# Two adds of a graph attention kernel move from VectorE to GpSimd

## The chip, the cores and the metric

The kernel runs on one core of a Trainium2 chip. A core has TensorE (PE: matmuls, with its weight loads shown apart as PEld), VectorE (DVE), ScalarE (ACT), GpSimd (POOL) and SyncE (SP, which here only issues DMAs). Each engine works through its own queue of instructions in order, and semaphores tie the queues together. The metric is the device time of one execution in microseconds; lower is better.

## The reference

Two graph layers are applied to 64 independent graphs of 256 nodes with 512 features, all in float32. Layer 0 is a one-head graph attention with a leaky ReLU; layer 1 is an 8-head attention whose scores carry a bias and the logarithm of the adjacency. Both add their input at the end.

```python
# layer 0
feat_proj = einsum('bnh,oh->bno', feats, fc_w) + fc_b
q = einsum('bnh,oh->bno', feat_proj, q_w) + q_b
k = einsum('bnh,oh->bno', feat_proj, k_w) + k_b
masked = q + swapaxes(k, 2, 1) + (1.0 - adj_mat) * -1e9
masked = where(masked >= 0, masked, 0.01 * masked)
x = einsum('bnm,bmh->bnh', softmax(masked), feat_proj) + feats
# layer 1: 8 heads of 64
Q, K, V = (x @ W + b for each of q, k, v)
scores = einsum('bihd,bjhd->bhij', Q, K) / sqrt(64)
a, c = x @ w_g[:D], x @ w_g[D:]
scores = scores + (a[:, :, None] + c[:, None, :] + b_g + log(adj + 1e-9))[:, None]
out = einsum('bhij,bjhd->bihd', softmax(scores), V) + x
```

## The kernel before, in words

The 64 graphs are taken in 32 groups of two (512 tokens). The work is a software pipeline of steps: in a step, group F goes through layer 0 and the projections of layer 1, group A, one older, goes through the attention of layer 1, group D, two older, finishes its last output, and the next group X loads and prepares its layer-0 weights. A steady step takes about 71 us. The order of instructions on each engine is written out by hand: `step` and `attention_and_layer_0` are lists of piece names, and each piece issues its instructions in that place. Nothing is reordered later; the framework only adds the semaphore waits that data and buffers need. PSUM has four single banks, `bank`, and two pairs of banks, `pair`, for the scores.

Weights of the softmax in layer 1 are made transposed (keys on partitions), for one graph `gr` and four heads at a time, which is a unit `u` = 0 to 3. A unit has two tiles `e[u, 0]` and `e[u, 1]`, one for each half of the keys, each 128 x 1024.

- `scores` (L859, L873): matmuls, then the exponential on ACT writes `e`.
- `factor` (L879): DVE multiplies `e` by adjacency + 1e-9, which stands for the logarithm in the scores.
- `both` (L886): the unit's two tiles are added into `esum`, the line that the change touches first.
- `parts` (L916, L917): DVE turns `esum` in blocks of 32 x 32 and reduces it to partial sums, so that the softmax needs no pass of its own. `totals` (L927) finishes the sums by a small matmul, `ratios` (L942, L951) takes reciprocals. In the last step of all, `sums_1` (L962) takes the sums for graph 0 by matmuls that read `esum` themselves.
- `attend` (L899, L906): matmuls of `e` with the values, copied to SBUF by ACT; `turn` (L991) transposes them on DVE, `divide` (L1011) multiplies by the reciprocals, `complete` (L1019) adds the residual with the bias, `xb`, and `store` (L1049) sends the tile out on SP's DMA queue. The last two outputs of the kernel go through `finish` (L1033 to L1040) in place of these.

Each of the large products (`pf` for layer 0, `pq`, `pk`, `pv` for layer 1) is a two-by-two block scheme with seven products instead of eight (L412), so sums of blocks precede and follow it. Its pieces `p1` to `p7` are matmuls, `keep_1` and the ends of `p6` and `p5` copy a bank to SBUF on ACT, and `sum_00` to `sum_11` are DVE instructions which read a PSUM bank and one SBUF tile (L443; for `pf` L501). The product `pf` is special (class `Mixed`): its kept tiles get the residual added on POOL (L495), the only steady work of POOL. The sums of token blocks are `ysum:0` to `ysum:3` for `pf` (L350, tiles `tb`, after ACT has copied `yT`, L695), and `xsum` for the others (L375). `keys`, `dot_q` and `dot_k` (L519) are dot products of the features with a vector; both inputs are in SBUF. `send` (L793, L797) and `fetch` (L805) transpose the result of layer 0 through DRAM. `load_x` (L206) loads the next group's features into the one buffer of x, after `keys` has read it.

The places of the two pieces in the order: `both:0` and `both:1` follow the factors of unit 1 and come before `ysum:0`; `both:2` comes after `turn:0` and `ratios:0`; `both:3` after the factors of unit 3 and before the `keys`. `complete:1` stands between `divide:1` and `store:1`, ahead of `ysum:1`; `complete:0` after the `dot_q`, with `store:0` and `parts:2` behind it:

```python
A("factor:1:0 factor:1:1 pv.sum_10 both:0 both:1")
F("mix:0 mix:1 ysum:0 recip")
D("ratios_of_all divide:1 complete:1 store:1")
A("residual:1")
F("mix:2 mix:3 ysum:1 ysum:2 ysum:3")
A("parts:0")
F("pf.p1 pf.keep_1 pf.p2 pf.p6 pf.sum_00 begin send:0:0 fetch:0:0")
```

The buffers concerned: `esum` has two, `e` six, `osb` two (shared with the turned tile of `parts:0`), `xb` two.

Of the kernel before, what the change touches and what calls it, by code (L numbers as in the profile page):

```python
# [13 lines left out]
ALU = mybir.AluOpType  # L14
# [11 lines left out]
def kernel(  # L26
# [64 lines left out]
    nc = tc.nc  # L91
# [72 lines left out]
    def fast():  # L164
        main = ExitStack()
        with main:
# [112 lines left out]
            def constant():  # L279

                both = two.tile([P, NC], F32, tag="c", name="qk_col")
                part = two.tile([P, 2, T], F32, tag="kq", name="qk_fcb")
                nc.vector.tensor_tensor(both, qw_col, kw_col, ALU.add)
                nc.vector.tensor_tensor(both, both, fcb_col, ALU.mult)
                nc.vector.tensor_reduce(part[:, 0, 0:1], both, AX.X, ALU.add)
                pk = bank("pk")
                nc.tensor.matmul(
                    pk[:, 0:1], lhsT=part[:, 0, 0:1].to_broadcast([P, P]), rhs=ones[:, 0, 0:1],
                    start=True, stop=True,
                )  # L290
                return lambda: nc.vector.scalar_tensor_tensor(
                    kqc, pk[:, 0:1], qb, kb, ALU.add, ALU.add
                )
# [235 lines left out]
            class Group:  # L529
# [353 lines left out]

                def both(self, u):
                    self.esum[u] = two.tile([P, 2, 2, N], F32, tag="es", name=f"es_{self.g}_{u}")
                    nc.vector.tensor_tensor(self.esum[u], self.e[u, 0], self.e[u, 1], ALU.add)  # L886

                def attend(self, gr):

# [126 lines left out]
                    )  # L1016

                def complete(self, gr):
                    nc.vector.tensor_tensor(self.osb[gr], self.osb[gr], self.xb[gr], ALU.add)  # L1019

                def ratios_t(self, gr):
                    self.st = one.tile([P, N], F32, tag="sms1", name=f"st_{self.g}_{gr}")
# [383 lines left out]
```

## Time and profile before

| what | us |
|---|---|
| time, median of 3 runs | 2311.84 (2310.98 to 2312.35) |
| span of the profiled execution, first to last instruction | 2308.8 |
| median less span | 3.0 |
| PE busy | 2294.2 (99%) |
| DVE busy | 2124.2 (92%) |
| ACT busy | 1071.8 (46%) |
| POOL busy | 121.9 (5%) |
| `both`, 126 on DVE | 149.3 |
| `complete`, 62 on DVE | 75.6 |

The profile is of one execution. A row of a group gives line, engine, operation, output and inputs by the program's tile names, shapes and count; then busy time in us and mean ns of one; then the idle time of the engine ahead of it and what ended most of it. A row of the timeline gives start and duration in us, engine, line and operation; a bracket is idle time before it with what ended it. A row of the waits says who waited for whom: total us, times, longest. DVE instructions overlap by some hundredths of a microsecond at their ends, and the ends of matmuls are modelled.

### The profile page before, as it was taken

Reading aid. Unit: us, or ns where it says so; the run is one execution under the profiler, and the core shown is the slowest. Engines: PE = TensorE matmul, PEld = TensorE weight load, DVE = VectorE, ACT = ScalarE, POOL = GpSimd, SP = SyncE. Lnnn points to the kernel's source line nnn. Section 1 sums busy time; section 2 is a strip of 40 time slices with the busy share of each in tenths; the row PEclk is TensorE's granted clock in tenths of the full one; section 3 lists DMA queues with packets and bytes.
Section 4 is the critical chain, followed back from the end, with each engine's and each line's share of the span. In section 5 each row is a group of like instructions: output and inputs, shape, how many; then the busy total and the mean of one; then the engine's idle time right before and its main releaser. Section 6 shows DMA issues by size and latency. Waiting matters only on the chain.

```text
span 2308.8 us, 33613 instructions
## 1 busy us (share of the span) xinstructions
PE 2294.2 (99%) x12618; PEld 1905.2 (83%) x12618; DVE 2124.2 (92%) x3180; ACT 1071.8 (46%) x1865; POOL 121.9 (5%) x120
## 2 busy tenths in 40 slices
PE   9999999999999999999999999999999999999997
PEld 6888888888888888888888888888888888888885
DVE  6899999999999999999999999999999999999997
ACT  3544444454445444454444454444544445444443
POOL 0000000000000000000000000000000000000000
PEclk9999999999999999999999999999999999999999
DMA  4122332223322233232233232332222323223312
GB/s 133 46 61 73 78 76 66 70 61 85 79 73 61 61 78 78 74 68 61 69 78 83 60 75 63 79 78 74 64 60 74 78 73 70 65 64 81 84 46 38
DMA packets 517264, 163.84 MB, mean 71 GB/s; under 512 B 415188, under 2 KB 478696, under 8 KB 517096
## 3 DMA queue, kind: packets, MB, share of 16 engines
q1 hardware_dynamic: 514440, 160.32, 28.8%
q8 instruction: 102, 1.67, 0.3%
q10 hardware_dynamic: 2656, 1.31, 0.2%
q14 instruction: 66, 0.54, 0.1%
HBM read 95.43 MB, written 66.12 MB: 70 GB/s over the span
## 4 chain that ended last, share of the span: by engine, by line
PE 98%; DVE 1%; DMA 0%; ACT 0%; issue 0%; ACTq 0%; DVEq 0%
PE pv L412 17%; PE pq L412 17%; PE pf L412 16%; PE pk L412 16%; PE sc L859 11%; PE oT L899 10%; PE y L689 9%; PE fp L718 1%; DMA fc_nat<-in_L_gnn_fc_w_dram 0%; PE rc L637 0%; DVE osb L1034 0%; PE tot L927 0%; DVE osb L1040 0%; PE xTp L705 0%; DVE osb L1033 0%; DVE x L756 0%
## 5 line engine op out<-in xcount | busy, mean ns | idle before, releaser
L873 ACT ACTIVATE e<-sc,c 128x1024 f32<-128x1024 f32 x254 | 269.0, 1110 | 79.2 <-PE sc L859 77.6
L879 DVE TENSOR_TENSOR e<-e,am 128x1024 f32<-128x1024 f32 x254 | 297.7, 1213 | 0.4 <-ACT e L873 0.4
L859 PE MATMUL sc<-qT,kT 64*128 64x256 f32 x2048 | 255.8, 390 | 0.3 <-ACT e L873 0.3
L899 PE MATMUL oT<-e,v 128*64 128x256 f32 x2032 | 233.4, 382 | 0.0
L859 PEld LDWEIGHTS sc<-qT,kT 64*128 64x128 f32 x2048 | 187.3, 187 | 52.6 <-issue 32.7
L495 POOL TENSOR_TENSOR pf_s<-pf_s,x 128x512 f32<-128x512 f32 x93 | 118.4, 1273 | 2106.1 <-ACT pf_s L494 2038.8
L689 PE MATMUL y<-e,x 128*128 128x256 f32 x992 | 225.6, 381 | 0.0
L899 PEld LDWEIGHTS oT<-e,v 128*64 128x64 f32 x2032 | 140.2, 137 | 85.3 <-issue 10.7
L689 PEld LDWEIGHTS y<-e,x 128*128 128x128 f32 x992 | 186.4, 190 | 23.7
L432 ACT ACTIVATE pq_s<-pq,cols 128x256 f32<-128x256 f32 x192 | 80.5, 470 | 249.1 <-PE pq L412 249.1
L494 ACT ACTIVATE pf_s<-pf,recip 128x256 f32<-128x256 f32 x186 | 77.9, 470 | 197.6 <-PE pf L412 197.6
L917 DVE TENSOR_REDUCE part<-est 128x32 f32<-128x1024 f32 x124 | 151.3, 1220 | 4.3
L916 DVE STREAM_TRANSPOSE est<-es 128x1024 f32<-128x1024 f32 x124 | 152.2, 1227 | 0.0
L886 DVE TENSOR_TENSOR es<-e,e 128x1024 f32<-128x1024 f32 x126 | 149.3, 1205 | 1.1
L695 ACT COPY yT<-y 128x512 f32<-128x512 f32 x124 | 72.6, 585 | 131.7 <-PE y L689 130.9
L429 ACT COPY pk_s<-pk 128x512 f32<-128x512 f32 x96 | 56.3, 586 | 165.7 <-PE pk L412 159.0
L906 ACT COPY oTs<-oT 128x512 f32<-128x512 f32 x128 | 75.0, 586 | 118.0 <-PE oT L899 97.3
L412 PE MATMUL pk<-t1b,wk 128*128 128x256 f32 x512 | 121.1, 380 | 0.4 <-DVE kT L443 0.4
L412 PE MATMUL pv<-wv,t1b_c 128*128 128x256 f32 x512 | 121.1, 380 | 0.0
L412 PE MATMUL pv<-wv,t1b 128*128 128x256 f32 x512 | 121.0, 380 | 0.0
L412 PE MATMUL pq<-x1T,wq 128*128 128x256 f32 x512 | 121.0, 379 | 0.0
L412 PE MATMUL pk<-x1T,wk 128*128 128x256 f32 x512 | 121.0, 379 | 0.0
(181 smaller groups left out, 4506.3 us busy)
## 6 DMA issues: line engine op xcount, KB each, us to landing
x<-in_x_dram SPq DMA_DIRECT2D x32, 1024.0 KB, 5.1
out_dram<-osb SPq DMA_DIRECT2D x254, 128.0 KB, 3.1
xd<-xt SPq DMA_DIRECT2D x124, 256.0 KB, 2.0
x1T<-xd SPq DMA_DIRECT2D x496, 64.0 KB, 1.9
adj<-in_adj_dram SPq DMA_DIRECT2D x128, 128.0 KB, 3.5
qrow<-q SPq DMA_DIRECT2D x31, 256.0 KB, 3.9
fc_nat<-in_L_gnn_fc_w_dram ACTq DMA_DIRECT2D x4, 256.0 KB, 3.8
wq<-in_L_gnn_W_q_dram SPq DMA_DIRECT2D x1, 1024.0 KB
```

Of the source, the lines that this page charges most:

```text
L412: nc.tensor.matmul(o, lhsT=lk[:, ts(m, P)] if len(lk.shape) == 2 else lk[:, m], rhs=rk, start=(start and m == 0 and k == 0), stop=(m == 1 ...
L432: nc.scalar.activation(dst[:, m], src[:, m], AF.Identity, bias=self.bias[:, 2 * o + m : 2 * o + m + 1],)
L494: nc.scalar.mul(s[:, m], src[:, m], self.recip[:, TPG * k + m : TPG * k + m + 1])
L495: nc.gpsimd.tensor_tensor(s, s, self.out(o, k), ALU.add)
L689: nc.tensor.matmul(y[:, ts(gr, N)], lhsT=self.x[:, gr * TPG + j, ts(c, P)], rhs=self.e0[:, j, gr, :], start=(gr == 0 and j == 0), stop=(gr ...
L859: nc.tensor.matmul(sc[:, par, pr, :], lhsT=self.kT[rows, 2 * hg + pr, ts(t, P)], rhs=self.qT[rows, 2 * hg + pr, ts(gr, N)], start=True, st ...
L873: nc.scalar.activation(e, sc, AF.Exp, bias=self.c[:, t : t + 1], scale=SCALE)
L879: nc.vector.tensor_tensor(ef, ef, self.am[:, jc, u // 2, :].unsqueeze(1).to_broadcast([P, 4, N]), ALU.mult,)
L886: nc.vector.tensor_tensor(self.esum[u], self.e[u, 0], self.e[u, 1], ALU.add)
L899: nc.tensor.matmul(oT[par * HD : (par + 1) * HD, pr, :], lhsT=self.v[:, gr * TPG + jc, ts(h, HD)], rhs=self.e[2 * gr + hg, jc][:, par, pr, :],
L916: nc.vector.transpose(turned, self.esum[u].rearrange("p a b i -> p (a b i)"))
L917: nc.vector.tensor_reduce(self.part[:, hg, :], turned.rearrange("p (m c) -> p m c", c=B), AX.X, ALU.add,)
```

## The change

Two method bodies issue their add on GpSimd and no longer on VectorE. Everything else, the order of the pieces included, stays. `both` then sits in POOL's queue among the three adds of `pf` in a step: POOL's order is `both:0`, `both:1`, `complete:1`, the three adds of `pf`, `both:2`, `both:3`, `complete:0`.

```diff
 def both(self, u):
     self.esum[u] = two.tile([P, 2, 2, N], F32, tag="es", name=f"es_{self.g}_{u}")
-    nc.vector.tensor_tensor(self.esum[u], self.e[u, 0], self.e[u, 1], ALU.add)
+    nc.gpsimd.tensor_tensor(self.esum[u], self.e[u, 0], self.e[u, 1], ALU.add)
...
 def complete(self, gr):
-    nc.vector.tensor_tensor(self.osb[gr], self.osb[gr], self.xb[gr], ALU.add)
+    nc.gpsimd.tensor_tensor(self.osb[gr], self.osb[gr], self.xb[gr], ALU.add)
```

## The prediction

> **What bounds the kernel now.** The page was read first: busy time and the chain that ended last.
>
> ```profile
> PE 2294.2 (99%) x12618; PEld 1905.2 (83%) x12618; DVE 2124.2 (92%) x3180; ACT 1071.8 (46%) x1865; POOL 121.9 (5%) x120
> PE 98%; DVE 1%; DMA 0%; ACT 0%; issue 0%; ACTq 0%; DVEq 0%
> ```
>
> TensorE (PE) never rests and nearly the whole chain is PE behind PE. VectorE (DVE) is at 92%, close enough to be taken for a partner bottleneck, so the waits of PE were read next. All of them together:
>
> ```profile
> PE pok L1096 <- DVE okp_last L1065: 5.0, 1, 5.0
> PE warm L1176 <- POOL ones L214: 1.5, 1, 1.5
> PE x1Tp L811 <- DVE x L756: 0.5, 1, 0.5
> PE pk L412 <- DVE kT L443: 0.4, 1, 0.4
> PE sc L859 <- ACT e L873: 0.3, 1, 0.3
> ```
>
> Each of these occurs once (total, times, longest). In the 31 steady steps of some 71 us PE waits for nobody; the 5.0 us at the end are for the range check. So shorter DVE work by itself is worth about nothing: what it could save is the single 0.4 us. A PE busy time may hide gaps, so the spacing was looked at too: 16 matmuls of the product pf start at 1012.80 and the next 16 at 1016.25, 216 ns each at a granted clock of 0.997, and the other products look the same. The question is therefore only whether the change makes DVE late enough for PE to wait, and the timeline of one steady step answers where the slack is small.
>
> The groups by shape give the prices:
>
> ```profile
> L886 DVE TENSOR_TENSOR es<-e,e 128x1024 f32<-128x1024 f32 x126 | 149.3, 1205 | 1.1
> L1019 DVE TENSOR_TENSOR osb<-osb,xb 128x1024 f32<-128x1024 f32 x62 | 75.6, 1220 | 1.1
> L495 POOL TENSOR_TENSOR pf_s<-pf_s,x 128x512 f32<-128x512 f32 x93 | 118.4, 1273 | 2106.1 <-ACT pf_s L494 2038.8
> ```
>
> [...]during the 93 POOL adds DVE runs transposes, a reduction and the PSUM-reading L501, which keep their usual 1.20 to 1.24 us and 0.47 us, and the adds take 1266 to 1292 ns. [...]no DVE instruction with two SBUF inputs lies under a POOL add for more than 0.08 us. [...]doubling the 1273 ns gives 2.55. I take 2.4.
>
> **The change, part by part.** DVE loses 126 x 1.205 + 62 x 1.220 = 225 us (7 us a step); POOL gains 188 x 2.4 = 451 us, so POOL is 25% busy and no bound. On PE's path the removal saves nothing, being hidden under PE. The moved instructions issue no DMA of their own, but `store` on SP waits for `complete`, and `parts` on DVE waits for `both`. Place by place in the step from 1000 us:
>
> `both:0`, `both:1`, `both:2`: the factors end at 1000.84, 1006.17 and 1029.28. POOL is busy 2.4 us after each, and DVE has then only transposes, a reduction, the PSUM sums or idle time (the next two-input work is at 1003.82, 1009.94 and 1034.38). No meeting, no cost. `parts:0` and `parts:1` come at 1015.57 and later, long after. The 2.3 us freed before 1009.94 become DVE idle time, because `ysum:0` waits for ScalarE's yT.
>
> `complete:1` is the expensive place:
>
> ```profile
> 1011.36 1.23 DVE L1011 TENSOR_TENSOR osb<-osb,recip 128x1024 f32<-128x1024 f32 x1
> 1012.62 1.22 DVE L1019 TENSOR_TENSOR osb<-osb,xb 128x1024 f32<-128x1024 f32 x1
> 1013.00 0.58 ACT L695 COPY yT<-y 128x512 f32<-128x512 f32 x1 [0.21 <-PE y L689]
> 1013.76 0.68 DVE L350 TENSOR_TENSOR tb<-yT,tb 128x512 f32<-128x512 f32 x1
> 1014.97 0.68 DVE L350 TENSOR_TENSOR tb<-yT,tb 128x512 f32<-128x512 f32 x1
> 1015.57 1.24 DVE L916 STREAM_TRANSPOSE est<-es 128x1024 f32<-128x1024 f32 x1
> 1015.64 1.27 POOL L495 TENSOR_TENSOR pf_s<-pf_s,x 128x512 f32<-128x512 f32 x1 [62.70 <-ACT pf_s L494]
> 1025.46 0.83 DVE L501 SCALAR_TENSOR_TENSOR x<-pf,recip,x 128x256 f32<-128x256 f32 x2
> 1028.68 0.26 PE L927 MATMUL tot<-part,every 128*64 128x32 f32 x4
> ```
>
> The division ends at 1012.59; 0.08 us later (the lag seen between ACT and the POOL add at 1015.64) POOL starts `complete:1` and holds the lock to 1015.07. `ysum:1` has its yT at 1013.58 and two SBUF inputs: it is held to 1015.07 and ends at 1015.75. Meanwhile the POOL add of `keep_1` has come at 1015.64. If waiters take turns, POOL goes next, 1015.75 to 1017.02; the remaining two sums then end at 1018.31 in place of 1015.65. From 1015.57 to 1026.29 DVE has no idle time, so all up to `sum_01` is late by 2.66 us: it ends at 28.95 instead of 26.29 (1000 us left out). The matmul of the totals, L927 at 28.68, writes the PSUM bank that `sum_01` has read (four banks; the other three are in use), so PE waits 28.95 - 28.68 = 0.27 us. The earlier waits hold: the second sum (slack 1.81 before the matmul at 1016.25), the third (2.93), and the first two attention banks (6.2 and 2.95). Behind L927 in PE's queue is everything, so the 0.27 us is lost each time. `complete:1` is run in 30 steady steps: 8.1 us. The removed `both:2` (1.2 us) and idle time then bring DVE back by 1034. SP stores from 1015.1 instead of 1013.87; its next issue is at 1019.74, no cost.
>
> `both:3` starts at 1038.70, while the `keys` (two SBUF inputs) run on DVE. One key goes first, POOL takes 2.4 us, the rest follow: the keys end near 1043.8 instead of 1042.7. The sum due after them at 1043.26 and one more of 0.68 us still end before DVE's next work, which waits for ScalarE until 1045.79, no cost; but the load of x starts 1.1 us later and the first `dot_q` can start at 49.5, not 48.39. By then `complete:0` has the lock (47.61 + 0.08 to 50.09), so `dot_q` starts at 50.09. From `dot_q` to the end of kT's sum is 1056.03 - 1048.39 - 1.13 (the gap left by L1019) = 6.51 us: it ends at 56.60.
>
> ```profile
> 1055.35 0.68 DVE L443 TENSOR_TENSOR kT<-pk,pk_s 128x512 f32<-128x512 f32 x1
> 1056.80 1.89 PE L412 MATMUL pk<-t1b,wk 128*128 128x256 f32 x8
> ```
>
> The matmul accumulates in the bank which that sum has read. Slack 0.77 before, 0.20 after: no stall, and none up to 2.6 us for a POOL add. The lateness of 0.6 us then lasts to the idle time at 1009 of the next step; the PE waits up to there have 2.4 us or more.
>
> Tail: the last step sums by matmuls of `esum`.
>
> ```profile
> 2280.08 1.23 DVE L886 TENSOR_TENSOR es<-e,e 128x1024 f32<-128x1024 f32 x1
> 2281.39 1.07 PE L962 MATMUL sm<-es,ones 128*32 128x256 f32 x16
> ```
>
> Slack 0.08. On POOL it runs from 2280.1 to 2282.5, 1.2 us later, and up to 2.0 if the lock held by `both:0` delays the second factor. I take 1.6.
>
> Sum on the profiled execution: 2308.8 + 8.1 + 1.6 = 2318.5. The median of the runs, 2311.84, is 3.0 above the span, so 2321.5.
>
> **Unknown costs from both sides.** [...]Taking turns: if DVE keeps the lock while it has instructions back to back, the sums end 1.4 us late, the stall is nil (below nothing is excluded: PE had no wait to lose). If each handover costs some tenths,[...] the stall is over 0.7 us a step.
>
> **Rivals.**
> Not slower: DVE's three sums go through back to back after `complete:1`, or reads interleave without a lock. DVE is 1.4 us late against the slack of 2.39 (28.68 - 26.29). It decides at the one handover at 1015.7: whether POOL's small add gets in between `ysum:1` and `ysum:2`. For it: DVE starts each instruction 0.07 us before its predecessor ends, so it may ask first. Against it: the POOL add is there at 1015.64, before `ysum:1` ends. Time 2308.8 + 1.6 + 3.0 = 2313.4.
> Much slower: a POOL add of 3 us or dear handovers. At 3 us the held sums are 3.3 us late (0.9 us at L927) and kT's sum 0.4 us past its slack: 30 x 1.3 = 39 us, about 2353. Against it: the very steady 1273 ns.
> Faster: DVE's freed 7 us a step are used. The profile has no PE wait on DVE there, so the gain is at most about 1 us: not worked out to a case of its own.
>
> **How the numbers follow.** Turns taken: 0.48. DVE keeps the lock or no lock: 0.37. Much slower: 0.11. Faster by something unseen: 0.04. About 0.2%, 4.6 us, is what a measurement can tell from no change. The second case lies within it, and so does a little of the first (stalls under 0.1 us): same 0.40, slower 0.56, faster 0.04. The range of 8 in 10 runs from just under the not-slower case, 2311, to a stall of 0.7 us a step, 2313.4 + 21 = 2334; within the likeliest case alone it is 2317 to 2328.
>
> **What would show it.** DVE's L350 (`tb<-yT,tb`) in part far longer than 0.68 us or with idle time before it that ends with POOL; L519 `jc` and `jq` likewise; POOL's L886 near 2.4 us; a wait of PE's tot L927 for DVE x L501, some 30 times 0.3 us; one for POOL es at L962 of 1 to 2 us. Wrong would be: no such wait (DVE keeps the lock), PE waits at kT L443 or at the third sum (handovers dearer than thought), or two-input DVE work that runs at its usual length under POOL (no lock).

## The result and the profile after

| | before | after |
|---|---|---|
| time, median (lowest to highest), us | 2311.80 (2310.98 to 2312.35) | 2333.14 (2332.50 to 2335.02) |
| profiled execution, us | | 2335.02 |
| its span, us | 2308.8 | 2333.2 |
| PE busy, us | 2294.2 | 2308.2 |
| DVE busy, us | 2124.2 | 2056.2 |
| POOL busy, us | 121.9 | 587.2 |

The change makes the kernel slower by 21.3 us: ratio 1.0095 with the interval 1.0080 to 1.0109. That is the foretold direction and inside the foretold range, but 2.2 times the 9.7 us that was forecast, and the stall is not where it was put. The profiled execution after the change is the longest of its four, 1.9 us above their median, so figures from the two traces add up to 24.4 us of span and not to 21.3.

The page after the change, busy time and the chain that ended last:

```profile
PE 2308.2 (99%) x12618; PEld 1896.2 (81%) x12618; DVE 2056.2 (88%) x2992; ACT 1072.8 (46%) x1865; POOL 587.2 (25%) x308
PE 71%; DVE 17%; DMA 6%; issue 2%; SPq 2%; ACT 1%; POOL 0%; DVEq 0%; ACTq 0%; POOLq 0%
```

PE still reads 99%. The chain tells more: it was 98% PE, and now about a quarter of it runs over DVE, DMA transfers and SP's queue. POOL itself has 0% of it. So the end is not set by adds on POOL that take long, but by something on DVE that has become late. Note also that DVE's busy time fell by 68 us only, where 225 us of adds left it.

The groups by shape say where most of the other 157 us are:

```profile
L886 POOL TENSOR_TENSOR es<-e,e 128x1024 f32<-128x1024 f32 x126 | 307.6, 2441 | 1281.5 <-DVE e L879 1281.5
L1019 POOL TENSOR_TENSOR osb<-osb,xb 128x1024 f32<-128x1024 f32 x62 | 146.2, 2358 | 285.3 <-DVE osb L1011 278.7
L495 POOL TENSOR_TENSOR pf_s<-pf_s,x 128x512 f32<-128x512 f32 x93 | 129.9, 1397 | 148.4 <-ACT pf_s L494 148.4
L519 DVE CUSTOM_DVE_ANT_0 jc<-x,wgc_row 128x512 f32<-128x512 f32 x128 | 151.1, 1180 | 3.3
L519 DVE CUSTOM_DVE_ANT_0 jq<-x,wq_row 128x512 f32<-128x512 f32 x128 | 103.8, 811 | 57.5 <-DMA x<-in_x_dram 54.2
L350 DVE TENSOR_TENSOR tb<-yT,tb 128x512 f32<-128x512 f32 x62 | 112.6, 1817 | 33.7 <-ACT yT L695 33.7
```

The add on POOL takes 2.36 us when nobody is in its way (2.4 was taken, an estimate of the author's). The DVE work with two SBUF inputs has grown: `tb<-yT,tb` from 684 to 1817 ns, the `keys` (`jc`) from 690 to 1180, the `dot_q` (`jq`) from 692 to 811: 70 + 63 + 15 = 148 us in all. As the timelines below show, the added time is a wait for POOL's add and not slower work: 1.95 us are recorded for a sum of 0.68, 2.72 for a key of 0.69. POOL's small add likewise went from 1273 to 1397 ns.

PE's waits after the change, those over 1 us in all, and one of its weight loads:

```profile
PE pok L1096 <- DVE okp_last L1065: 5.0, 1, 5.0
PE sm L962 <- POOL es L886: 2.6, 1, 2.6
PE pk L412 <- ACT pk_s L429: 2.2, 6, 0.7
PE pk L412 <- DVE kT L443: 2.0, 6, 0.3
PE warm L1176 <- POOL ones L214: 1.5, 1, 1.5
PE pq L412 <- ACT pq_s L432: 1.4, 5, 0.3
PE pq L412 <- DVE t1b L375: 1.1, 3, 0.6
...
PEld pk L412 <- DVE kT L443: 10.7, 22, 0.7
```

There is no wait of PE at the totals (L927), where the forecast put 0.27 us in each step. PE waits instead in the projections `pq` and `pk`. These rows add up to less than what was lost, because the modelled ends of matmuls hide part of the gaps. A better measure is to pair each matmul with itself in the trace of before and see by how much its start has moved. Steps 2 to 30 lose 18.8 us in this way: 7.7 at `pk.p4`, behind kT's sum; 4.5 at `pq.p3` and 4.2 at `pk.p3`, behind tiles that ACT could not keep in time (ACT's `pk_s` waits 119.8 us in all for DVE's sum for qT, 6.6 before); 2.2 at `pq.p6`, behind `xsum`; 0.3 at `pq.p4`, nothing at the totals. The last step loses 5.1. This shift is what "PE lost" means below.

**The first meeting.** The timeline of the step that the prediction used (7.11 us later in this trace, counted from the first matmul of `pf`):

```profile
1018.47 1.22 DVE L1011 TENSOR_TENSOR osb<-osb,recip 128x1024 f32<-128x1024 f32 x1
1019.78 2.35 POOL L1019 TENSOR_TENSOR osb<-osb,xb 128x1024 f32<-128x1024 f32 x1 [2.90 <-DVE osb L1011]
1020.73 1.95 DVE L350 TENSOR_TENSOR tb<-yT,tb 128x512 f32<-128x512 f32 x1 [1.03 <-ACT yT L695]
1022.61 0.68 DVE L350 TENSOR_TENSOR tb<-yT 128x512 f32<-128x512 f32 x1
1022.75 1.66 POOL L495 TENSOR_TENSOR pf_s<-pf_s,x 128x512 f32<-128x512 f32 x1 [0.62 <-ACT pf_s L494]
1023.21 1.75 DVE L350 TENSOR_TENSOR tb<-yT,tb 128x512 f32<-128x512 f32 x1
1024.88 1.23 DVE L916 STREAM_TRANSPOSE est<-es 128x1024 f32<-128x1024 f32 x1
```

`ysum:1` takes 1.95 us instead of 0.68: it stands behind `complete:1`. `ysum:2` goes next, since the small add arrives only at 1022.75, when `ysum:2` has begun; the small add then takes 1.66 instead of 1.27 and goes ahead of `ysum:3`, which is held to 1.75. So they did take turns, one whole instruction each, in order of arrival, in every one of the 30 steady steps with the same figures. That is what "the lock" stands for here: DVE work with two inputs in SBUF that met an add on POOL was held until the add had ended, or nearly. The trace of before has no such meeting longer than 0.08 us, so in the prediction it was the author's assumption. DVE's other work kept its length under POOL's adds after the change too: the transposes `est<-es` took 1.20 to 1.24 us there, the reductions `part<-est` 1.22, the sums `v<-pv,pv_s`, which read PSUM, 0.68 to 0.69. `parts:0` starts 2.20 us late, not 2.66: the lock was free about 0.13 us before POOL's recorded end (`ysum:1` needs 0.68 us and ends at 1022.68, so it got the lock at 1022.00; `complete:1` is recorded until 1022.13). The slack at the totals was 2.39, so 0.19 of it is left and PE does not wait there.

**What the lateness becomes.** The same step further on. First three rows of before, `xsum:0`, the second key and the first `dot_q`:

```profile
1034.38 0.65 DVE L375 TENSOR_TENSOR t1b<-x1T 128x512 f32<-128x512 f32 x1
...
1040.53 0.69 DVE L519 CUSTOM_DVE_ANT_0 jc<-x,wgc_row 128x512 f32<-128x512 f32 x1
...
1048.39 0.69 DVE L519 CUSTOM_DVE_ANT_0 jq<-x,wq_row 128x512 f32<-128x512 f32 x1 [0.78 <-DMA x<-in_x_dram]
```

Then the rows after the change, DVE with the POOL and SP rows that belong to it:

```profile
1042.52 0.69 DVE L375 TENSOR_TENSOR t1b<-x1T 128x512 f32<-128x512 f32 x1 [0.95 <-DMA x1T<-xd]
...
1047.45 2.72 DVE L519 CUSTOM_DVE_ANT_0 jc<-x,wgc_row 128x512 f32<-128x512 f32 x1
...
1057.06 0.96 DVE L519 CUSTOM_DVE_ANT_0 jq<-x,wq_row 128x512 f32<-128x512 f32 x1 [2.02 <-DMA x<-in_x_dram]
...
1063.16 0.68 DVE L443 TENSOR_TENSOR kT<-pk,pk_s 128x512 f32<-128x512 f32 x1
...
1046.95 2.67 POOL L886 TENSOR_TENSOR es<-e,e 128x1024 f32<-128x1024 f32 x1 [5.86 <-DVE e L879]
1055.11 2.36 POOL L1019 TENSOR_TENSOR osb<-osb,xb 128x1024 f32<-128x1024 f32 x1 [5.49 <-DVE osb L1011]
...
1051.81 0.40 SPq L206 DMA_DIRECT2D x<-in_x_dram  x1
```

Medians over 29 steady steps, in us from the first matmul of `pf` in the step:

| point | before | after | later by |
|---|---|---|---|
| `parts:0` starts | 2.77 | 4.98 | 2.21 |
| first `send` issued | 6.95 | 9.15 | 2.20 |
| third `send` issued | 14.27 | 16.47 | 2.20 |
| `xsum:0` starts | 21.58 | 22.60 | 1.02 |
| `keys` end | 29.89 | 31.71 | 1.82 |
| load of x issued | 30.04 | 31.86 | 1.82 |
| first `dot_q` starts | 35.29 | 37.25 | 1.96 |
| last `dot_q` ends | 38.18 | 40.68 | 2.50 |
| kT's sum ends | 42.93 | 44.30 | 1.37 |

This table shows the way that the lateness takes, and each difference has its place. The sends go out 2.20 us late, because they follow the sums on DVE. DVE itself then catches up, as foretold, but it has to wait at `xsum:0` for what SP's queue brings back through DRAM (the 0.95 us of idle time in the first line), and 1.02 us of lateness come out there. At the keys 1.20 us of removed `both:3` stand against 2.03 us for which the second key is held (2.72 less 0.69): 0.83 more. The load of x waits for the keys and hands the 1.82 on. The first `dot_q` gets 0.27 us more from the lock of `complete:0` in this step. The removed `complete:0` gives 1.13 back. The time that a transfer takes from issue to landing is the same before and after in the median (sends 2.0 us, fetches 1.9 and 2.0); it is the start that is late.

**Which steps lose.** The medians don't show where the cost arises. The slack at kT's sum, 0.77 us in the step that the prediction read, has a median of 1.07 in the trace of before (0.08 to 1.26), and after the change the steps differ widely in what they lose:

| steps | number | `xsum:0` starts | first `dot_q` takes, median | PE lost |
|---|---|---|---|---|
| with a range check | 7 | 22.33 to 23.93 | 2.16 | 10.2 |
| others, `xsum:0` late | 9 | 22.83 to 24.19 | 0.92 | 7.8 |
| others | 13 | 22.25 to 22.65 | 0.87 | 0.8 |

In the steps without a check PE loses what the start of `xsum:0` goes beyond 22.5 us, within 0.1 us in 21 of 22 steps: nothing at 22.44, 0.65 at 23.16, 1.67 at 24.19. In each of the nine late ones a single issue of a send or fetch on SP takes 0.66 to 1.85 us, where most take 0.3 to 0.5. Such slow issues are not new: before the change they are there in 12 of the 29 steps, but `xsum:0` starts at 22.04 at the latest. Step 27, before and then after:

```profile
1949.01 4.71 SPq L805 DMA_DIRECT2D x1T<-xd  x8
1955.78 0.65 DVE L375 TENSOR_TENSOR t1b<-x1T 128x512 f32<-128x512 f32 x1
...
1967.53 5.35 SPq L805 DMA_DIRECT2D x1T<-xd  x8
1974.71 0.69 DVE L375 TENSOR_TENSOR t1b<-x1T 128x512 f32<-128x512 f32 x1 [2.53 <-DMA x1T<-xd]
```

Before, the fetches had some 1.2 us of room ahead of `xsum:0` (2.20 of lateness at the sends gave 1.02 there), and slow issues vanished in it. The late sends have used this room up, and in the steps with a slow issue PE now loses. This is read from the traces and was not tested by itself; nor is it known why an issue is slow. The steps with a check have another reason, shown with e6.

**The tail.** The timeline of the last step:

```profile
2296.34 3.20 POOL L886 TENSOR_TENSOR es<-e,e 128x1024 f32<-128x1024 f32 x1 [4.26 <-DVE e L879]
2300.77 2.34 POOL L886 TENSOR_TENSOR es<-e,e 128x1024 f32<-128x1024 f32 x1 [1.23 <-DVE e L879]
2303.16 1.08 PE L962 MATMUL sm<-es,ones 128*32 128x256 f32 x8 [2.61 <-POOL es L886]
```

In the trace of before, PE's sixteen matmuls of L962 run from 2281.39 without a gap. Now PE waits for the second tile of `esum`, as foretold, but for 2.61 us. The first add has to let a factor on DVE go ahead (3.20 us recorded, 2.36 of them its own), then holds the next factor for as long, so that the second add can't start before 2300.77. Counted from the scores' matmuls just before (2277.54 in the trace of before, 2296.06 here), that is 2.2 us later than before, and the add itself is 1.1 us longer. Paired with before, PE loses 3.0 us at these matmuls. It loses 2.7 more over the next 6 us, without waiting: the granted clock of PE is 0.50 there (2303 to 2309), and 1.00 at the same place before (2283 to 2290). Some 0.7 us that had been lost earlier come back ahead of the two, which leaves the 5.1. That the wait brings the halved clock is not shown: in e6 PE has the same wait of 2.6 us and loses 2.0 us in its last step, not 5.1.

### The profile page after: what moved, and what is told of

The parts are those of the page before. It is cut to its first block, busy times and chain, and to the rows that moved or that the text cites. A ratio compares the mean times of both kernels' runs of the same rounds, so it can differ in the third digit from the quotient of the medians.

```text
span 2333.2 us, 33920 instructions
## 1 busy us (share of the span) xinstructions
PE 2308.2 (99%) x12618; PEld 1896.2 (81%) x12618; DVE 2056.2 (88%) x2992; ACT 1072.8 (46%) x1865; POOL 587.2 (25%) x308
## 3 DMA queue, kind: packets, MB, share of 16 engines
q8 instruction: 102, 1.67, 0.3%
## 4 chain that ended last, share of the span: by engine, by line
PE 71%; DVE 17%; DMA 6%; issue 2%; SPq 2%; ACT 1%; POOL 0%; DVEq 0%; ACTq 0%; POOLq 0%
PE pv L412 15%; PE pk L412 11%; PE pf L412 10%; PE y L689 9%; PE pq L412 9%; PE sc L859 8%; PE oT L899 7%; DMA x<-in_x_dram 3%; DVE jc L519 3%; SPq L805 2%; DVE jq L519 2%; DVE tb L350 2%; DVE e L879 2%; DVE est L916 2%; DVE x L501 2%
## 5 line engine op out<-in xcount | busy, mean ns | idle before, releaser
L886 POOL TENSOR_TENSOR es<-e,e 128x1024 f32<-128x1024 f32 x126 | 307.6, 2441 | 1281.5 <-DVE e L879 1281.5
L1019 POOL TENSOR_TENSOR osb<-osb,xb 128x1024 f32<-128x1024 f32 x62 | 146.2, 2358 | 285.3 <-DVE osb L1011 278.7
L495 POOL TENSOR_TENSOR pf_s<-pf_s,x 128x512 f32<-128x512 f32 x93 | 129.9, 1397 | 148.4 <-ACT pf_s L494 148.4
L519 DVE CUSTOM_DVE_ANT_0 jq<-x,wq_row 128x512 f32<-128x512 f32 x128 | 103.8, 811 | 57.5 <-DMA x<-in_x_dram 54.2
L519 DVE CUSTOM_DVE_ANT_0 jc<-x,wgc_row 128x512 f32<-128x512 f32 x128 | 151.1, 1180 | 3.3
L350 DVE TENSOR_TENSOR tb<-yT,tb 128x512 f32<-128x512 f32 x62 | 112.6, 1817 | 33.7 <-ACT yT L695 33.7
L429 ACT COPY pk_s<-pk 128x512 f32<-128x512 f32 x96 | 56.2, 586 | 187.0 <-DVE qT L443 119.8
L412 PE MATMUL pq<-t1b,wq 128*128 128x256 f32 x512 | 121.2, 379 | 0.0
```

The source lines that it names most:

```text
L350: nc.vector.tensor_tensor(s[:, n], *sums[n], ALU.subtract)
L412: nc.tensor.matmul(o, lhsT=lk[:, ts(m, P)] if len(lk.shape) == 2 else lk[:, m], rhs=rk, start=(start and m == 0 and k == 0), stop=(m == 1 ...
L519: nc.vector.tensor_tensor_reduce(out=junk, in0=src, in1=w_row, scale=1.0, scalar=init, op0=ALU.mult, op1=ALU.add, accum_out=dst,)
L886: nc.gpsimd.tensor_tensor(self.esum[u], self.e[u, 0], self.e[u, 1], ALU.add)
L1019: nc.gpsimd.tensor_tensor(self.osb[gr], self.osb[gr], self.xb[gr], ALU.add)
```

## The experiments

Three explanations were held against each other. The chain theory, formed from the table of medians above: `complete:1` makes the sums late, and the lateness travels through sends, fetches, keys and the load of x to kT's sum, where only what exceeds the slack is lost. The adding theory: every moved add costs its own share in its own place. The theory of late results: work on POOL simply ends later, and its readers wait for it.

The runs with their ratio to the kernel before, how much later kT's sum ends than before (median of 29 steps), and what PE lost in steps 2 to 30 and in the last step:

| run | time, us | ratio (95%) | kT later | PE lost |
|---|---|---|---|---|
| after | 2333.14 | 1.0095 (1.0080 to 1.0109) | 1.37 | 18.8 + 5.1 |
| e1, only `both` on POOL | 2317.70 | 1.0027 (1.0015 to 1.0038) | 0.88 | 2.8 + 2.0 |
| e2, only `complete` on POOL | 2324.56 | 1.0051 (1.0034 to 1.0067) | 1.00 | 12.1 + 0.0 |
| e3, `both:3` back | 2322.10 | 1.0043 (1.0028 to 1.0057) | 0.88 | 7.9 + 3.8 |
| e4, `complete:1` back | 2314.57 | 1.0010 (1.0003 to 1.0017) | 0.69 | 1.8 + 1.4 |
| e5, only `both:0` to `both:2` on POOL | 2311.79 | 1.0003 (0.9994 to 1.0012) | | 0.0 + 0.0 |
| e6, after without the range checks midway | 2324.51 | 1.0057 (1.0040 to 1.0074) | 0.98 | 9.2 + 2.0 |
| e7, last step's adds back | 2330.06 | 1.0078 (1.0062 to 1.0095) | | 18.7 + 0.0 |
| e8, `complete:1` two pieces later | 2327.99 | 1.0072 (1.0055 to 1.0089) | 0.97 | 11.6 + 4.9 |
| e9, `complete:1` only writes | 2313.46 | 1.0009 (1.0002 to 1.0016) | 0.69 | 1.7 + 0.4 |
| e10, keys ahead of `both:3` | 2323.05 | 1.0054 (1.0037 to 1.0070) | 0.42 | 6.9 + 3.8 |
| e11, before with half a reduction more | 2314.69 | 1.0014 (1.0007 to 1.0021) | 0.79 | 2.0 + 1.0 |
| e12, before with a reduction more | 2328.78 | 1.0077 (1.0060 to 1.0094) | 1.33 | 15.5 + 2.0 |

Each ratio is against executions of the kernel before made together with that run. The chain theory's numbers were right in e5, e11 and e12 and within 0.6 us in e6, e7 and e9; they were 1 to 2.5 us off in e1, e3, e4 and e10, and 7.6 and 10.0 us too low in e2 and e8. They had been worked out with the slack of 0.77 and one step for all. What the misses have in common can be read step by step: how far kT's sum ends beyond the moment at which the matmul behind it started before, added up over steps 2 to 30, is 15.7 us after the change, 9.2 in e2, 10.3 in e8, 5.1 in e10 and 11.1 in e12, to which some 0.15 us come for each step in which PE waits. That comes within 1 us of what PE lost in each of these runs; it is bookkeeping of the traces and no test of its own.

**One kind of add alone: e1 and e2.** Each leaves the other kind on DVE.

```diff
 # e1: from after
-nc.gpsimd.tensor_tensor(self.osb[gr], self.osb[gr], self.xb[gr], ALU.add)
+nc.vector.tensor_tensor(self.osb[gr], self.osb[gr], self.xb[gr], ALU.add)
 # e2: from after
-nc.gpsimd.tensor_tensor(self.esum[u], self.e[u, 0], self.e[u, 1], ALU.add)
+nc.vector.tensor_tensor(self.esum[u], self.e[u, 0], self.e[u, 1], ALU.add)
```

> Only both moves to GpSimd; complete stays on VectorE. Chain theory (the lock makes VectorE late at three places, the lateness adds up along the order of the step, and TensorE waits only for what exceeds the slack of 0.77 us at kT's sum): the keys are held 2.0 us by both:3, x is loaded 1.1 us later, and complete:0 (1.2 us) stands in VectorE's path again behind it, so 0.3 us a step are over the slack: 2320 to 2328 us. Adding theory (each meeting costs TensorE its own share of the steady 18.8 us, in proportion to how long it holds VectorE: complete:1 with the small add 2.3 us, both:3 2.0, complete:0 0.3): 8 us and the tail, 2323 to 2326. GpSimd-late theory (nothing is held, those who read esum or send osb get it late): as the changed kernel without the stores, about 2330.

> Only complete moves to GpSimd; both stays on VectorE. Chain theory: the block sums are 2.2 us late, the keys 1.0, the load of x 1.0, dot_q starts when complete:0 gives way, and kT's sum is 0.6 us late, inside the slack: 2313 to 2317 us. Adding theory: 10.6 us, 2322 to 2325. GpSimd-late theory: about 2316.

In e1 the sums keep their old length (685 ns) and the keys are held as in the full change (1181 ns); in e2 it is the other way round, 1836 and 690. The two cost 6.1 and 12.9 us against the kernel before run with them, 2311.62, and together they make 19.0 of the 21.3. That alone would fit the adding theory, and e2 lies in the range expected from it and above the chain theory's: with `complete` alone PE loses 12.1 us, and a new wait shows whose lateness it is, that of a transfer:

```profile
PE pq L412 <- DMA x1T<-xd: 2.9, 4, 0.9
```

**Which place: e3, e4 and e5.**

```diff
 # e3
+(nc.vector if u == 3 else nc.gpsimd).tensor_tensor(self.esum[u], ...)
 # e4
+(nc.vector if gr == 1 else nc.gpsimd).tensor_tensor(self.osb[gr], ...)
 # e5: complete on DVE altogether, and
+(nc.vector if u == 3 or self.g == NG - 1 else nc.gpsimd).tensor_tensor(self.esum[u], ...)
```

> The changed kernel with both:3 alone back on VectorE. Chain theory: the keys are no longer held, all steady steps but those with the range check fit into the slack; tail of 5 us stays: 2317 to 2321 us. Adding theory: 8 us less than the changed kernel, 2325 to 2328. GpSimd-late theory: no difference, 2333.

> The changed kernel with complete:1 alone back on VectorE. Chain theory: the block sums, the fetch and the keys start in time, the keys are held once, kT's sum is 0.5 to 0.7 us late, inside the slack but for the steps with the range check; most of the tail stays: 2317 to 2322 us. Adding theory: 9 us less than the changed kernel, 2324 to 2327. GpSimd-late theory: 2330 to 2333.

> Only both:0, both:1 and both:2 of the groups 0 to 30 move to GpSimd, the three places that meet no VectorE work with two SBUF inputs. Chain theory: none held, VectorE is freed of 3.6 us a step that nobody waits for: 2309 to 2314 us, no difference to the kernel before. GpSimd-late theory: some 2 us a step of lateness for those who read esum, but off TensorE's path: 2312 to 2318. That the freed VectorE time is used after all: under 2308.

e4 decides against the adding theory. With `complete:1` back the time falls by 18.6 us, to 2314.57. With `both:3` back it falls by 11.0. These two sum to 29.6 of the 21.3 that were there, so the parts can't be independent: they share one slack. The traces show the sharing. In e3, of the 18 steps without a check that start `xsum:0` by 23.15 us, 14 lose nothing, and the four that start it later lose what goes beyond some 23.3 us. The limit had been 22.5; it has moved by about what the hold of the keys had taken, 0.8. In e4 `xsum:0` is back at 21.58 us, the keys end at 30.66 (0.77 late), and the lock of `complete:0` sets the rest: kT's sum is 0.69 late, which is under the median slack of 1.07, and only 1.8 us are lost. That is nearly what the prediction had worked out for this place, 0.57.

e5 answers two questions at once. `both:0`, `both:1` and `both:2` on POOL cost nothing, as foretold; and the DVE time that they free, 3 x 1.2 us in a step, is worth nothing: the ratio is 1.0003. Its chain that ended last is like that of the kernel before:

```profile
PE 98%; DVE 1%; DMA 0%; ACT 0%; issue 0%; SPq 0%; DVEq 0%
```

**The lock itself: e9.** In place of `complete:1` POOL writes the same tile three times without reading SBUF; the residual of the second graph is lost, and its output with it. POOL is then busy for about as long, but with writes only.

```diff
 def complete(self, gr):
+    if gr == 1:
+        nc.gpsimd.memset(self.osb[gr], 0.0)
+        nc.gpsimd.memset(self.osb[gr], 0.0)
+        nc.gpsimd.memset(self.osb[gr][:, 0:512], 0.0)
+        return
```

> The changed kernel with complete:1 made of three memsets on GpSimd (1024, 1024 and 512 elements a partition, some 2.4 us), which write the output tile and read no SBUF; the outputs of the second graph of each group are zero, the division and the residual for them are lost. If the lock is one of reads[...]: the block sums keep 0.68 us and the small add 1.27, 2314 to 2318 us. If any GpSimd instruction holds VectorE: sums of up to 1.95 us as in the changed kernel, 2328 to 2335.

The groups of e9:

```profile
L350 DVE TENSOR_TENSOR tb<-yT,tb 128x512 f32<-128x512 f32 x62 | 42.7, 688 | 33.7 <-ACT yT L695 33.7
L1020 POOL MEMSET osb<- 128x1024 f32 x31 | 29.5, 951 | 109.2 <-DVE osb L1011 109.2
L495 POOL TENSOR_TENSOR pf_s<-pf_s,x 128x512 f32<-128x512 f32 x93 | 118.3, 1272 | 154.8 <-ACT pf_s L494 154.8
```

The sums are back at 688 ns and the small add at 1272, and 19.7 us of the loss are gone, although `store:1` still waits for POOL and POOL is busy for 2.43 us in place of 2.36 (951, 951 and 524 ns for the three memsets). So it is not POOL's lateness that costs, but the add that reads SBUF: this rules the theory of late results out for `complete:1`. The three memsets, which only write, did not hold the two-input sums.

**Another order: e8.** `complete:1` with its store was put behind the copy of the kept tile, so that the sums on DVE run before it.

```diff
-D("ratios_of_all divide:1 complete:1 store:1")
+D("ratios_of_all divide:1")
 ...
-F("pf.p1 pf.keep_1 pf.p2 pf.p6 pf.sum_00 begin send:0:0 fetch:0:0")
+F("pf.p1 pf.keep_1")
+D("complete:1 store:1")
+F("pf.p2 pf.p6 pf.sum_00 begin send:0:0 fetch:0:0")
```

> The changed kernel with complete:1 and store:1 moved in the written order from behind divide:1 to behind pf.keep_1, so that GpSimd does the small add first and complete:1 runs under the transposes, the reduction and the PSUM sums of VectorE; it is as late in GpSimd's queue as 4 us. Chain theory (the held block sums are the root): the sums keep 0.68 us, 2314 to 2318 us, as where complete:1 is back on VectorE, 2314.6. GpSimd-late theory (the output tile and its four stores come late): 2333 or more.

The sums are clear of the lock (0.69, 0.68 and 0.69 us in the step from 1012 us of its trace), and yet 2327.99 is far above the 2314 to 2318 that the chain theory gave. SP's rows of e8 say why:

```profile
1022.99 2.80 SPq L1049 DMA_DIRECT2D out_dram<-osb  x4
1025.89 0.63 SPq L797 DMA_DIRECT2D xd<-xt  x1
1028.60 1.75 SPq L805 DMA_DIRECT2D x1T<-xd  x4
```

The four stores are now issued from 1022.99, and the first send, whose data was ready at 1023.3, stands behind them in SP's queue until 1025.89. The medians agree: the first send goes out at 9.36 us of the step (6.95 before), `xsum:0` at 22.45, kT's sum 0.97 late. The expectation had looked at DVE alone; the lateness took the other way into the same transfers. It is a miss for the kernel and support for the route: a delay of the sends by another cause made `xsum:0` late too.

**Away from the keys: e10.** The keys and the load of x were moved ahead of the third unit's factors and `both:3`.

```diff
-A("factor:3:0 factor:3:1 both:3")
 F("keys:2 keys:3 keys:0 keys:1")
 X("load_x")
+A("factor:3:0 factor:3:1 both:3")
```

> The changed kernel with keys and load_x moved in the written order ahead of factor:3 and both:3. The block sums are still held by complete:1, but the keys no longer wait behind factor:3 and both:3, so x is loaded some 4 us earlier. If the lateness reaches TensorE by the way keys, load of x, dot_q, sum of kT: 2316 to 2321 us (the tail stays). If it reaches TensorE by the late fetch and the block sums of x1 alone, or at the totals: 2328 to 2334.

The keys are back at 690 ns, but the meeting has moved on to the `dot_q`, which no longer wait for a transfer:

```profile
L519 DVE CUSTOM_DVE_ANT_0 jq<-x,wq_row 128x512 f32<-128x512 f32 x128 | 149.5, 1168 | 3.4
```

What PE loses in the steady steps falls from 18.8 to 6.9 us, and the time lands slightly above the 2316 to 2321 expected. At 0.42 us kT's sum is within its slack in the median step, and 6.2 of the 6.9 us lie in the steps with a range check.

**The range checks: e6.** In seven steps midway DVE also checks ranges, with 1.65 us of instructions ahead of `divide:0`; e6 leaves those checks out.

```diff
 def check():
+    return
```

> The changed kernel without the range checks in the middle of the run (seven steps; only the last groups are checked, so the fallback could not be told for the others). In the changed kernel TensorE loses 1.0 to 1.5 us in each of these seven steps and some 0.4 us in the others. Chain theory (the check's 1.7 us of VectorE come on top of the lateness and go over the slack in full): 5 to 8 us less, 2325 to 2328 us. If the check has nothing to do with it: 2332 to 2334.

The time falls by 8.6 us. In the full change a step with a check loses 1.0 to 2.6 us, 10.2 in the seven; in e6 the same seven lose 1.9. It is not that they had less slack: before the change their kT's sum ends at 42.76 us in the median, earlier than in the others (42.98), since the check runs in idle time of DVE ahead of the `dot_q`. After the change DVE comes late to the check, `divide:0` starts at 34.96 us in place of 33.91 in the other steps, and `complete:0` behind it at 36.26 in place of 35.20. So its lock is still held when x has landed, and the first `dot_q` is held for some 1.45 us and not 0.2. Step 9, before and then after:

```profile
693.46 0.69 DVE L519 CUSTOM_DVE_ANT_0 jq<-x,wq_row 128x512 f32<-128x512 f32 x1
...
700.34 2.14 DVE L519 CUSTOM_DVE_ANT_0 jq<-x,wq_row 128x512 f32<-128x512 f32 x1 [0.85 <-DMA x<-in_x_dram]
```

In e6 this `dot_q` takes 0.95 us in these steps. The prediction had taken one step for all 31.

**The tail: e7.** The two `both` of the last group and the two `complete` of the group before it, all in the last step, went back to DVE.

```diff
+(nc.vector if self.g == NG - 1 else nc.gpsimd).tensor_tensor(self.esum[u], ...)
+(nc.vector if self.g >= NG - 2 else nc.gpsimd).tensor_tensor(self.osb[gr], ...)
```

> The changed kernel with the adds of the last step (both of group 31, complete of group 30) back on VectorE. If the 5.1 us that TensorE loses in the last step come from them: 2328 to 2330 us. If the last step only inherits lateness from the steps ahead: 2332 to 2334.

3.1 us between the medians, 5.1 in the shift of PE; the steady steps keep their 18.7. The tail is a cost of its own and adds.

**The slack without POOL: e11 and e12.** To the kernel before, and with nothing on POOL changed, a useless reduction on DVE was added after `parts:2`, that is between the `dot_q` and kT's sum; half of one (512 elements) in e11, a whole one in e12.

```diff
 # e12, in parts, behind the reduction
+if u == 2:
+    nc.vector.tensor_reduce(
+        self.part[:, hg, :],
+        turned.rearrange("p (m c) -> p m c", c=B), AX.X, ALU.add,
+    )
```

> The kernel before, with nothing on GpSimd, and one reduction of 512 elements more on VectorE (0.69 us, repeating half of parts:2) ahead of kT's sum. If lateness up to the slack of 0.77 us is free: 2311 to 2315 us. If each us of lateness there costs TensorE at once: 31 x 0.69 = 21 us, 2333.

> The same with the reduction of parts:2 repeated whole, 1.22 us. By the slack of 0.77 us: 31 x 0.45 = 14 us, 2322 to 2330 us, with the waits at the matmul behind kT's sum. If VectorE's idle 8% takes it in: 2312. If it costs in full: 38 us, 2350.

In both, the transfers are on time (`xsum:0` at 21.58 us). 0.79 us of lateness cost 3.2 us in the median, 1.33 us cost 17.3. So there is a slack at kT's sum as the prediction had said, though 0.77 us was its size in one step and not in all, and what goes beyond it is paid. PE's wait in e12 is at the same sum, here without any lock:

```profile
PE pk L412 <- DVE kT L443: 9.3, 17, 1.7
```

None of the versions beats the kernel before; e5 equals it. With PE at 99% and its gaps already closed, there was no wait that a freer DVE could have removed.

## Why the prediction was right and wrong

**The bound, right.** PE bounds the kernel and DVE's freed time is worth nothing. e5 shows it: 1.0003.

**The price of the add, right.** 2.36 us alone, against the 2.4 taken. That was the author's estimate: the trace of before had 1273 ns for an add of 512 elements, and twice that is 2.55.

**The lock and the turns, right in kind.** Two-input work on DVE was held for a whole POOL add (1.95 us recorded for a sum of 0.68), and the waiters took turns. The first rival, that DVE keeps the lock and ends within the measurement of no change, fell with it; under memsets on POOL, which read no SBUF, the sums kept their 688 ns (e9). The size was a little off: 2.20 us late instead of 2.66. 0.18 of the difference is `complete:1` letting go earlier (aligned 1014.89 against 1015.07), the rest the same early release at the small add and the overlap of DVE's starts. The order of the turns was not quite the one foretold. At the handover that was to decide, `ysum:1` had ended (1015.57, aligned) before the small add came at 1015.64, so `ysum:2` went next, as the rival had it; the add got in one sum later, and the lateness came out nearly the same. That much of the agreement is luck.

**The stall at the totals, wrong.** It was 2.66 - 2.39 = 0.27 us, 8.1 in 30 steps; measured 2.20 - 2.39, so nothing. A difference of two near numbers decided the sign, and the lateness was taken 0.46 us too long. That the total still came out in the foretold range is luck as well: the 8.1 us stood for a stall that did not come.

**The step that failed: "The removed `both:2` (1.2 us) and idle time then bring DVE back by 1034".** DVE did come back; its data did not. The sends had left 2.2 us late, and they return through DRAM by fetches on SP, so that `xsum:0` finds its data 1.02 us late. The prediction followed the lateness along one engine's queue and stopped where that queue had idle time; it named "all up to `sum_01`" as late and did not follow the sends that those results start. Hence the sum at kT came out as 0.57 us late and free within 0.77, where 1.37 was measured in the median and up to 3.7 in single steps. A wait at kT's sum had been named as a sign of handovers dearer than thought; it came, but no cost of handovers shows at the first meeting, where the lock was even free 0.13 us early. With `complete:1` back on DVE (e4) the prediction's own working of this place holds: 0.69 against 0.57, and nearly nothing lost. That this is the route, and not only its end, rests on e4, e9 and e8: take away the hold on the sums and `xsum:0` is on time again; delay the sends in another way and it is late again. And without a check PE loses step for step what `xsum:0` starts after 22.5 us. How the 18.8 us divide among the single waits of `pq`, `pk` and `pv` was read from the trace and not tested one by one. Nor was it tried what a faster way for the transfers would give back.

**Left out of the sum.** The other readers of this lateness, since ACT's kept tiles wait for qT's sums (8.7 us at `pq.p3` and `pk.p3`), and the differences between steps: in those with a range check `complete:0` holds the first `dot_q` for longer (8.6 us by e6), and in nine others a slow issue on SP comes on top. These are parts of the same 18.8.

**`both:0` to `both:2` free, the store free, right.** e5 for the former. For the store, e9 leaves at most its 2.1 us for all that remains, the store's wait for POOL among it.

**The tail, right in kind, mis-sized.** 1.6 us were taken, at most 2.0; 3.1 in the medians of e7 and 5.1 in the trace, where 2.7 of it falls in the time of the halved clock, which the prediction did not have. The upper bound had the right cause, the second factor held by the first add, but counted 0.8 us for it where the second add starts 2.2 us late.

**The time around the span.** It was taken as 3.0 us, from one span and a median of other runs. The profiled execution itself took 2335.02 with a span of 2333.2, so 1.8; the forecast was 1.2 us too high there.

The forecast sum of 8.1 + 1.6 us on the span stands against 24.4 measured; the products `pq` and `pk`, put at zero, lost 18.8 of them.

## What to carry to other kernels

Ask of each instruction that becomes late what it starts, not only what stands behind it in its own queue: here sends that left 2.20 us late brought `xsum:0` its data 1.02 us late through DRAM, though DVE had idle time in between. The adds on POOL held the DVE work with two SBUF inputs that they met (0.68 us became 1.95, and 0.69 became 2.72), as if they stood in DVE's queue, so search the timeline for each such meeting; moved adds which met no such work cost nothing here (e5, 1.0003). And do not take one step, or the median, for all. Here a spare 1.2 us ahead of `xsum:0` had swallowed slow transfer issues that no wait of the profile before showed, and the steps with a check had more slack than the others until DVE came late to it; these two kinds of step lost 18 of the 18.8 us.

## What the runs showed of the hardware that was not expected

- At this meeting the lock was given in order of arrival, one instruction at a time, with the same result in all 30 steps (1.95, 0.68 and 1.75 us for the sums, 1.66 for POOL's add); and it was free some 0.13 us before POOL's recorded end, taking the held sum's own time as its usual 0.68.
- Here a recorded duration contained the wait for the lock. A key of 0.69 us shows as 2.72, so a mean of 1180 ns in a group is one held instruction out of four and not slower work.
- One issue of a send or fetch on SP at times takes 0.6 to 1.9 us where most take 0.3 to 0.5, in 12 of 29 steps before the change and in 16 after it, counted ahead of `xsum:0`. Its cause is open.
- POOL instructions that only write (memsets of 128 x 1024, 0.95 us) did not hold DVE's two-input sums: 688 ns in the mean with three of them in place of `complete:1`, 1817 with the add.
